# Register loads behind each block's turn, late sums at iterations' ends, rows stored by position, and first splits of layer 1 amid the last gates, in a two-layer routed network on one core

## The chip, the cores and the metric

The kernel runs on one core of a Trainium2 chip. The core has a matmul engine (TensorE, in the profile PE, with PEld for its weight loads), three engines for elementwise work (VectorE = DVE, ScalarE = ACT, GpSimd = POOL), and a queue that only issues transfers (SyncE = SP). ACT and POOL issue transfers too. Each engine executes its instructions in order, and waits for others by semaphores. The metric is the device time of one execution in microseconds, lower is better; the time of the kernel before is the median of 3 runs.

## The reference

The input x has 32 sequences of 128 rows with 512 values; there are two layers, each x + ffn(cond(x)). Cut to what matters:

```python
# layer 0, cond: a mixture of experts with top-2 routing
shared = (silu(x @ sw1.T) * (x @ sw3.T)) @ sw2.T            # hidden width 1024
s      = sigmoid(x @ router_w.T + (t_emb @ router_t_w.T)[seq])
top2   = top_k(s + router_bias, 2)                          # of 8 experts
hidden = (shared + sum(gate_e * gelu(x @ rw1[e].T) @ rw2[e].T)) / 3
# layer 0, ffn: one of 8 experts for each sequence
sel    = argmax(softmax(gelu(hidden[:, -1] @ Wp1 + bp1) @ Wp2 + bp2))
x      = x + hidden + 0.3 * ((gelu(hidden @ W1[sel] + b1[sel]) @ W2[sel] + b2[sel]) @ Wo + bo)
# layer 1, cond: 16 experts by a hash of the token, 256 places each
xk, xr = x + dxprev * maa_k, x + dxprev * maa_r             # dxprev: row before minus row
y      = expert_out[slot];  expert_out = relu(xk_rows @ w_key[e])**2 @ w_value[e]
z      = sigmoid(xr @ w_recept) * y
# layer 1, ffn: a gated recurrence over the 32 sequences (128 rows side by side)
f, i, g = sigmoid(z@wf.T+c@uf.T+bf), sigmoid(z@wi.T+c@ui.T+bi), tanh(z@wc.T+c@uc.T+bc)
c      = f * c + i * g                                       # 32 steps
x      = x + tanh(z @ wo.T + c @ uo.T + bo)
```

## The kernel before

All of it is one program. Matrix products in float32 are made of three matmuls in a reduced format: each operand is split into a high part, a copy on ACT (L64), and a low part, a subtraction on DVE (L65, `split`), and `mm3` (L82) adds high x high, high x low and low x high in PSUM. So every operand passes through ACT and then DVE before PE can use it, and both do this in program order.

The framework schedules the instructions of each engine by priorities and releases; `tc.issue_after(x)` holds an instruction behind instruction x in that schedule, and `behind(pair)` does so for two. `value_load` and `values_load` read a number from SBUF into a register of an engine; it is an instruction on that engine's queue and is shown in no row of busy time. The stages, with the times of the profiled execution:

- 0 to 300 us, shared experts of sequence groups 0 to 3 (8 groups of 4 sequences, 512 columns). `shared` runs 8 chunks of the hidden width for each group: `up` makes two products, `down` adds to 4 accumulators. `mid0` is called after each half of a chunk of group 0 (half steps m = 2n + w) and puts the router's matmuls among them: `cut(m)` says how many of the 32 pieces of x the router has done by then (4 pieces of group 0, 28 that are fetched again by `fetch_r` and split). `seq_bias` computes the routing bias by sequence; its condition `n + w == 1` holds for two half steps, so it runs twice. Then the generators `slots` (places for layer 1's experts) and `choose` (top 2, block tables) advance a step for each chunk from `hook2`. Loads of x and of weights are issued on SP by `fetch`.
- 300 to 548 us, routed experts: 64 full blocks of 128 gathered rows and up to 7 more in conditional pairs (`maybe`, from block 16 on, every sixth block). For block i `r_up` multiplies with a matrix whose column is a register, `first_col(i)`, read by PE from blk_e; `turn_x(i + 1)` transposes the next rows, `r_down(i - 1)` is the second product, `turn_h(i)` the transpose between (L682). The count of used blocks is read by four engines at block 12 (`used`), and each conditional (L702) branches on it. `maybe` reads the columns of its pair in front of the branch.
- 548 to 827 us, shared experts of groups 4 to 7. Beside them `get_o(b)` gathers the two expert rows of sequence b and loads its shared rows (shc) and x, and `combine(b)` adds them up (L793, L794), transposes (L797) and stores the hidden rows. After 24 sequences `policy` picks each one's expert and sorts the sequences by it: seq_i is the sequence at each position, idxw the weight rows.
- 827 to 1431 us, the second product of layer 0 by position. Iteration b runs `up`, `bend` (transpose and gelu) and `down` for two halves of the hidden width, `turn_r`, and for each pair of positions `close` (the product with Wo, new x, and xk). `send_k` and `send_v` transpose and store xk rows and gate rows r = xr @ w_recept to xk_d and v_d, at the row of the sequence, for which SP or ACT reads seq_i into a register (`rows_of`). Weights are gathered on POOL (L906), split on ACT and DVE only where the expert changes (a conditional on a register, L934). The last four sequences are summed in here: `get_o` at b = 3, 6, 9, 12, `combine` at b = 5, 8, 11, 14, both in the middle of the iteration, the second `policy` for positions 24 to 31 at b = 17.
- 1431 to 1809 us, layer 1's experts: 16 experts of 8 weight pieces. `fetch_piece` loads a piece on SP (L1321), `split_piece` splits it, `fetch_rows` gathers an expert's xk rows by slot_t on POOL (L1335), `turn_rows` transposes them (L1348), `use_piece` multiplies; the last piece copies the result on ACT (L1382) and stores it to res_d from ACT's queue (L1384).
- 1809 to 2495 us, the recurrence, 32 steps of about 20.0 us. `get_y(b)` gathers y from res_d on POOL (L1456) and loads r from v_d on SP (L1461); `gate_y` multiplies (L1476) and transposes (L1481). Weights come through `weight` (L1426). After the last step the outputs are finished group by group, without matmuls from 2473.7 us on.

The sequence of each conditional in the routed stage, before:

```python
es = [first_col(i) for i in pairs[n]]
with tc.If(used > pairs[n][0]):
    for i, e in zip(pairs[n], es):
        r_up(i, e)
```

Of the kernel before, what the change touches and what calls it, by code (L numbers as in the profile page):

```python
# [20 lines left out]
P = 128  # L21
# [4 lines left out]
GB = 4  # L26
# [23 lines left out]
def tile_kernel(ctx: ExitStack, tc: tile.TileContext, a: dict, out: bass.AP):  # L50
# [44 lines left out]
    bias_d = dram.tile([E0 * P, 3 * KD], F32, tag="bias", name="bias_d")  # L95
    v_d = dram.tile([N, D], F32, tag="v", name="v_d")
    sh_d = dram.tile([(NG // 2 + 1) * GT, D], F32, tag="sh", name="sh_d")
    o_d = dram.tile([NBLK * P, D], F32, tag="o", name="o_d")
    xk_d = dram.tile([N, D], F32, tag="xk", name="xk_d")
# [31 lines left out]
    seq_i = const.tile([P, NB], I32, name="seq_i")  # L131
    s0_i = const.tile([P, NB], U32, name="s0_i")
# [17 lines left out]
    pad = const.tile([P, 416 // 4], F32, name="pad")  # L150
# [7 lines left out]
    with ExitStack() as sa:  # L158
# [6 lines left out]
        def fetch(src, name):  # L165
            t = raw_p.tile([P, D], F32, tag="raw", name=name)
            nc.sync.dma_start(out=t, in_=src)
            return t

# [35 lines left out]
        def fetch_x(g):  # L205
            if g < NG:
                x_raw[g] = [fetch(a["x"][g][:, k, :], f"xraw_{g}_{k}") for k in range(KD)]
# [68 lines left out]
        with ExitStack() as s0:  # L276
# [32 lines left out]
            fetch_sw(1)  # L309
            ps_acc = s0.enter_context(tc.tile_pool(name="ps_acc0", bufs=4, space=PSUM, **kw))  # L310
# [51 lines left out]
            def seq_bias():  # L362

                ps = ps_r.tile([P, NB, E0], F32, tag="r", name="ps_tb")
                for k in range(KD):
# [7 lines left out]
                    mm(ps, ones, pr, k == 0, k == KD - 1)  # L373
# [4 lines left out]
            def fetch_r(i):  # L378
                g, k = divmod(i, KD)
                if 0 < g < NG:  # L380
                    xrs[i] = fetch(a["x"][g][:, k, :], f"xr_{g}_{k}")
# [165 lines left out]
            def slots():  # L547
# [28 lines left out]
                yield from invert(slot_t, [hi], [lo], NSLOT // P, "st")  # L576
                zero = rtile([P, D], "zero")
# [15 lines left out]
            def cut(m):  # L593
                return min(NR, KD + (NR - KD) * (m - 1) // 15) if m > 0 else 0

            def mid0(n, w):

                if n < KF:
# [3 lines left out]
                    for i in range(cut(m + 1), cut(m + 2)):  # L602
                        fetch_r(i)
                    if n + w == 1:
                        seq_bias()
# [3 lines left out]
            def hook2(g, c):  # L609

                if g == 0:
                    next(steps[0], None)
                    return
                if g == 1 or (g == 2 and c < 5):
# [40 lines left out]
        with s1:  # L655
# [4 lines left out]
            last_up = []  # L660
# [4 lines left out]
            def r_up(i, e=None):  # L665
                if e is None:
                    with tc.issue_after(last_up[0]) if last_up else nullcontext():
                        e = first_col(i)
                x = xb.pop(i)
                pu = ps_u.tile([P, HR], F32, tag="u", name=f"pur_{i}")  # L670
                last_up[:] = [
# [6 lines left out]
            def turn_h(i):  # L678
                u, e = us.pop(i)
                pt = ps_h.tile([P, HR // P, P], F32, tag="t", name=f"pth_{i}")  # L680
                for k in range(HR // P):
                    nc.tensor.transpose(pt[:, k, :], u[:, bass.ts(k, P)], ident)  # L682
# [4 lines left out]
            def r_down(i):  # L687
                h, e = hb.pop(i)
                po = ps_o.tile([P, D], F32, tag="o", name=f"por_{i}")
                mm3(po, lambda q, k: h[:, q, k, :], lambda q, k: r2[:, q, bass.ds(e + k * D, D)], HR // P)  # L690
# [9 lines left out]
            def maybe(n):  # L700
                es = [first_col(i) for i in pairs[n]]
                with tc.If(used > pairs[n][0]):  # L702
                    for i, e in zip(pairs[n], es):
                        r_up(i, e)
# [7 lines left out]
                last_up.clear()  # L712

            for i in range(NFULL + 1):
                if i < NFULL:
# [7 lines left out]
                if i < NFULL:  # L723
                    turn_h(i)
                n, step = divmod(i - FIRST, STEP)
                if i == FIRST - 4:
                    engines = (nc.tensor, nc.scalar, nc.vector, nc.sync)
                    used = nc.values_load(
                        used_i[0:1, 0:1], engines=[x.engine for x in engines], min_val=NFULL, max_val=NBLK
                    )  # L730
# [38 lines left out]
        for kind, i in BIAS.items():  # L769
            nc.sync.dma_start(out=bias_d[:, bass.ts(i, KD)], in_=a[kind][:, KD * D :])  # L770
# [42 lines left out]
        def policy(b0, b1, sm, ps_t, room=None):  # L813
# [69 lines left out]
            nc.vector.tensor_scalar(idxw[:, b0:b1], srow, part_f, None, ALU.add)  # L883
# [900 lines left out]
```

## Time and profile before

| | us |
|---|---|
| median of 3 runs | 2500.74 |
| lowest and highest | 2498.92, 2503.20 |
| profiled execution, own time | 2497.22 |
| its span | 2495.5 |
| PE busy | 2434.5 |
| PEld, DVE, ACT, POOL busy | 2060.7, 1326.8, 1034.5, 412.3 |

The profile comes from one execution; its mean granted TensorE clock is 0.991 of full speed. A row of the waits names an engine, the work that waited and what ended the wait, with total, count and longest in us. A row of the timeline gives start and length of a run of like instructions, and in brackets the idle time in front of it. A row of the windows gives the busy time of each engine in a stretch, and behind it the granted clock.

### The profile page before, as it was taken

To read this page: it belongs to the slowest core of one execution; us is meant where nothing else is said; L and a number is where in the kernel's file an instruction comes from. 1 tells how busy PE (TensorE), PEld (TensorE's weight loads), DVE (VectorE), ACT (ScalarE), POOL (GpSimd) and SP (SyncE) were. 2 spreads that over 40 slices of the span, in tenths; PEclk is the share of its full clock that TensorE was granted. 3 is DMA by queue.
4 is the path that set the end of the run, shared out by engine and by line. 5 is a ranking of instruction groups with operands and counts; after the bars stand their busy time and mean duration, and the time that the engine had idled before them with its cause. 6 is when DMAs were issued, how large, how long until landed. Compare 5 with 4: busy or idle time off the path is not lost.

```text
span 2495.5 us, 36566 instructions
## 1 busy us (share of the span) xinstructions
PE 2434.5 (98%) x12932; PEld 2060.7 (83%) x12932; DVE 1326.8 (53%) x2265; ACT 1034.5 (41%) x1826; POOL 412.3 (17%) x462
## 2 busy tenths in 40 slices
PE   8999999999999899999999999999999999999996
PEld 5788888888888788888888889999978888888885
DVE  7897644456567344454454486766642333333336
ACT  4444533343224454454454376666532222222214
POOL 1000022221233233322222100000010000000003
PEclk9999999999999999999999999999999999999998
DMA  5545544457564333341342487777431111111017
GB/s 181 168 126 169 187 161 161 163 185 238 183 215 165 115 120 127 102 153 57 118 146 94 152 295 232 222 228 234 155 125 39 38 40 42 43 42 38 26 70 280
DMA packets 193402, 351.62 MB, mean 141 GB/s; under 512 B 37504, under 2 KB 72368, under 8 KB 190144
## 3 DMA queue, kind: packets, MB, share of 16 engines
q1 hardware_dynamic: 142080, 246.51, 29.9%
q0 software_dynamic: 36448, 75.95, 10.3%
q10 hardware_dynamic: 14688, 26.75, 3.0%
q8 instruction: 108, 1.77, 0.3%
q14 instruction: 78, 0.64, 0.1%
HBM read 373.94 MB, written 88.65 MB: 185 GB/s over the span
## 4 chain that ended last, share of the span: by engine, by line
PE 49%; DVE 2%; DMA 1%; ACT 0%; issue 0%; POOL 0%; SPq 0%; POOLq 0%; DVEq 0%; ACTq 0%
PE phD L82 7%; PE ps_c L82 7%; PE ps_f L82 7%; PE ps_i L82 7%; PE poD L82 7%; PE poF L82 3%; PE po L82 3%; PE pb L82 2%; PE pv L82 1%; PE ptF L1481 1%; PE ptC L1488 1%; PE ptD L1348 0%; DMA v_d<-r 0%; DMA rawD<-in_w_value_dram 0%; PE ptB L1196 0%
## 5 line engine op out<-in xcount | busy, mean ns | idle before, releaser
L65 DVE TENSOR_TENSOR wD<-rawD,wD 128x1024 fp32r<-128x1024 f32 x128 | 156.4, 1229 | 80.8 <-ACT wD L64 80.7
L82 PE MATMUL p<-xhl,swu 128*128 128x512 f32 x768 | 188.7, 397 | 6.5 <-ACT xhl L64 6.5
L82 PE MATMUL phD<-xe,wD 128*128 128x256 f32 x1536 | 186.9, 282 | 2.0 <-DVE hf L1367 2.0
L82 PEld LDWEIGHTS phD<-xe,wD 128*128 128x128 f32 x1536 | 186.0, 190 | 3.3 <-issue 2.2
L82 PE MATMUL p<-xhl,kept_u 128*128 128x512 f32 x768 | 184.3, 394 | 0.7 <-DVE kept_u L65 0.7
L82 PE MATMUL poD<-wD,hD 128*128 128x512 f32 x768 | 181.3, 392 | 0.0
L82 PEld LDWEIGHTS p<-xhl,swu 128*128 128x128 f32 x768 | 144.6, 190 | 36.9 <-ACT xhl L64 6.5
L82 PEld LDWEIGHTS p<-xhl,kept_u 128*128 128x128 f32 x768 | 141.9, 188 | 30.0 <-DVE kept_u L65 1.1
L82 PEld LDWEIGHTS poD<-wD,hD 128*128 128x128 f32 x768 | 142.0, 188 | 28.4
L64 ACT CAST wD<-rawD 128x1024 fp32r<-128x1024 f32 x128 | 133.2, 1047 | 55.4 <-PE poD L82 50.1
L281 POOL DMA_INDIRECT xg<-in_x_rows_dram,blk_t x71 | 67.6, 952 | 454.9 <-PE ptx L291 246.4
L1456 POOL DMA_INDIRECT y<-res_d,gat_i x32 | 30.8, 962 | 573.6 <-DVE r L1476 492.1
L82 PE MATMUL pur<-r,xb 128*128 x792 | 111.5, 291 | 7.2 <-issue 4.2
L82 PE MATMUL por<-r,hbr 128*128 x396 | 108.0, 407 | 1.2 <-ACT hbr L64 1.2
L82 PEld LDWEIGHTS pur<-r,xb 128*128 128x128 f32 x792 | 99.7, 192 | 9.0 <-issue 6.9
L65 DVE TENSOR_TENSOR xb<-ptx,xb 128x512 fp32r<-128x512 f32 x68 | 47.0, 691 | 106.4 <-ACT xb L64 104.7
L82 PE MATMUL poF<-z,wo_hl 128*128 128x512 f32 x384 | 96.4, 399 | 0.0
L82 PE MATMUL ps_f<-wf_hl,z 128*128 128x512 f32 x384 | 96.2, 399 | 0.0
L82 PE MATMUL ps_c<-wc_hl,z 128*128 128x512 f32 x384 | 94.7, 396 | 0.7 <-ACT z L64 0.7
L82 PE MATMUL pb<-rT,Wo_hl 128*128 128x256 f32 x768 | 94.7, 281 | 0.3 <-DVE rT L65 0.2
L82 PE MATMUL acc<-swd,as 128*128 128x512 f32 x384 | 95.0, 392 | 0.0
L82 PE MATMUL pv<-w_recept_hl,xr 128*128 128x512 f32 x384 | 93.1, 391 | 0.5 <-ACTq L934 0.4
(1017 smaller groups left out, 4955.6 us busy)
## 6 DMA issues: line engine op xcount, KB each, us to landing
rawD<-in_w_key_dram SPq DMA_DIRECT2D x64, 512.0 KB, 4.3
rawD<-in_w_value_dram SPq DMA_DIRECT2D x64, 512.0 KB, 4.4
swr<-in_sw_dram SPq DMA_DIRECT2D x120, 256.0 KB, 3.2
o_d<-obr SPq DMA_DIRECT2D x66, 256.0 KB, 2.4
xraw<-in_x_dram SPq DMA_DIRECT2D x32, 256.0 KB, 4.2
rraw<-in_rw_dram SPq DMA_DIRECT2D x32, 256.0 KB, 3.0
xc<-in_x_dram SPq DMA_DIRECT2D x32, 256.0 KB, 3.5
hid_d<-o ACTq DMA_DIRECT2D x32, 256.0 KB, 2.2
```

The lines of the kernel that those rows point to most:

```text
L64: first = nc.scalar.copy(hi, src).ins
L65: done = nc.vector.tensor_tensor(lo, src, hi.bitcast(F32), ALU.subtract).ins
L82: done = nc.tensor.matmul(ps, lhsT=left(hl, k), rhs=right(hr, k), start=start and k + n == 0, stop=stop and 3 * k + n == last,)
L281: nc.gpsimd.indirect_dma_start(out=xg[i], out_offset=None, in_=a["x_rows"], in_offset=bass.IndirectOffsetOnAxis(ap=blk_t[:, i : i + 1], ax ...
L1456: got = nc.gpsimd.indirect_dma_start(out=y, out_offset=None, in_=res_d, in_offset=bass.IndirectOffsetOnAxis(ap=gat_i[:, b : b + 1], axis=0),)
L1481: nc.tensor.transpose(pt[:, k, :], r[:, bass.ts(k, P)], ident)
L1488: nc.tensor.transpose(pt[:, k, :], c[:, bass.ts(k, P)], ident)
```

## The change

- Start: the three loads to bias_d go from the start of the third stage's code (where the schedule issued the first of them at 3.63 us) to group 1, behind the weight loads there. Pieces 0 and 2 of the first x are loaded from ACT's queue. The router's pieces have buffers of their own and are fetched behind the first loads; `cut` starts two half steps later and ends at the same one (13 instead of 15). `seq_bias` runs once, at the end of group 0, and adds its four products on DVE ahead of a single matmul.
- Routed blocks: `know(i)` reads the column of block i behind block i - 1's transposes (`turn_h`), no longer behind its first product; the loads of `used` stand behind the second product and split of the blocks before 12, and those of a conditional's pair inside the branch, each behind the block before it.
- Late sums: `get_o` is issued behind the hid and weight loads of its iteration, `combine` and `policy` go to the end of the iteration, behind the last split and the last transposes; the second policy comes at b = 15.
- Rows by position: `send_k` and `send_v` store at the position's fixed row, with no register. Layer 1's gather list slot_t is corrected for it: `policy` keeps pos_i and moved = (position - sequence) x 128, and `by_position`, at b = 16 and 17, adds to each entry of slot_t the move of its sequence (slot_b). In the recurrence r is loaded from a row that SP reads from pos_i, one load behind the other.
- Seam to layer 1: the pools for its pieces and rows open before the end of the stage before; 6 pieces are fetched and the first rows gathered there, and five pieces are split on ACT and DVE before the last gate products (two of them ahead of the mix of the last positions). On ACT the casts of wc and wi then come ahead of the last two result copies (L1382) in the instruction order.

```diff
+                    if c == KF - 1:
+                        seq_bias()
...
+                    if k > 0:
+                        nc.vector.tensor_tensor(pr, pr, sum_, ALU.add)
+                    sum_ = pr
+                ps = ps_r.tile([P, NB, E0], F32, tag="r", name="ps_tb")
+                mm(ps, ones, sum_, True, True)
...
-                return min(NR, KD + (NR - KD) * (m - 1) // 15) if m > 0 else 0
+                return min(NR, KD + (NR - KD) * (m - 3) // 13) if m > 2 else 0
...
+            def know(i, *behind):
+                with ExitStack() as order:
+                    for ins in behind:
+                        order.enter_context(tc.issue_after(ins))
+                    cols[i] = first_col(i)
...
-                es = [first_col(i) for i in pairs[n]]
+                last_pe.clear()
                 with tc.If(used > pairs[n][0]):
-                    for i, e in zip(pairs[n], es):
-                        r_up(i, e)
+                    for i in pairs[n]:
+                        know(i, *last_pe)
+                        r_up(i)
...
+                if i + 1 < NFULL:
+                    know(i + 1, *last_pe, *(loads[:1] if i == FIRST - 3 else ()))
...
+        def by_position(pool, i):
+            n = D // NB
+            for s in (bass.ts(i, n),):
...
+                nc.vector.tensor_tensor(
+                    room, slot_b[:, s].unsqueeze(2).to_broadcast([P, n, NB]),
+                    iota_b.unsqueeze(1).to_broadcast([P, n, NB]), ALU.is_equal,
+                )
+                nc.vector.tensor_tensor(room, room, moved.unsqueeze(1).to_broadcast([P, n, NB]), ALU.mult)
...
+                nc.vector.tensor_reduce(by, room, AX.X, ALU.add)
+                nc.vector.tensor_tensor(slot_t[:, s], slot_t[:, s], by, ALU.add)
...
-            return t[bass.ds((seq(p, queue) + where(p)[0] * PARTS[0]) * P, P), :]
+            return t[p * P : (p + 1) * P, :]
...
+                with tc.issue_after(last_hid[0]), tc.issue_after(last_w[0]):
+                    get_o(NB - GB + late, cb, 1)
...
-            if 0 <= late < GB and step == 2:
-                combine(NB - GB + late, ps_t)
-            if late == GB and step == 2:
-                policy(PARTS[0], NB, cb, ps_t)
...
                 bend(b + 1, "b")
+                with behind(last_split), tc.issue_after(last_turn[0]):
+                    if 0 <= late < GB and step == 2:
+                        combine(NB - GB + late, ps_t)
+                    if late == GB and step == 0:
+                        policy(PARTS[0], NB, cb, ps_t)
+                    if late == GB and step > 0:
+                        by_position(cb, step - 1)
...
+        AHEAD, RAW, FIRST = 8, 6, 5
+        fetch_rows(0)
+        for p in range(RAW):
+            fetch_piece(p)
+        fetch_rows(1)
+        for p in range(2):
+            with behind(r_done):
+                split_piece(p)
+            fetch_piece(p + RAW)
+        with tc.issue_after(last_piece[0]):
+            store_x1(NB // PB - 1, 1)
...
+        for p in range(2, FIRST):
+            with behind((r_done[0], xr_done)):
+                split_piece(p)
+            fetch_piece(p + RAW)
...
-            nc.sync.dma_start(out=r, in_=v_d[b * P : (b + 1) * P, :])
+            with tc.issue_after(last_r[0]):
+                at = nc.sync.value_load(pos_i[0:1, b : b + 1], min_val=0, max_val=PARTS[part] - 1)
+            last_r[:] = [nc.sync.dma_start(out=r, in_=v_d[bass.ds((at + part * PARTS[0]) * P, P), :]).ins]
```

## The prediction

> **What bounds the kernel now.** I read the page's busy times first, then TensorE's waits, then the timeline and the windows around each wait.
>
> ```profile
> span 2495.5 us, 36566 instructions
> PE 2434.5 (98%) x12932; PEld 2060.7 (83%) x12932; DVE 1326.8 (53%) x2265; ACT 1034.5 (41%) x1826; POOL 412.3 (17%) x462
> ```
>
> TensorE (PE) is busy for all but 61.0 us. Some 22 us of these are the tail after its last matmul at 2473.7, which the change leaves alone. So a gain can come from three places only: the other 39 us of idle time, matmuls that are no longer issued, and matmuls that ran at half clock. The waits, by what PE waited for (total, times, longest):
>
> ```profile
> PE po L82 <- DVE hb_0a L65: 6.7, 1, 6.7
> PE p L82 <- ACT xhl L64: 6.5, 1, 6.5
> PE pur L82 <- issue: 4.2, 1, 4.2
> PE ptD L1348 <- DMA rowsD<-xk_d,slot_t: 2.4, 2, 1.4
> PE ptF L1481 <- DVE r L1476: 2.3, 1, 2.3
> PE phD L82 <- DVE hf L1367: 2.0, 1, 2.0
> PE pur L82 <- PEq L702: 1.9, 1, 1.9
> PE rt L56 <- DVE rwa L359: 1.8, 1, 1.8
> PE ps_tb L56 <- ACT zt L397: 1.7, 1, 1.7
> PE ps_tb L56 <- DVE tbias L374: 0.8, 1, 0.8
> ```
>
> Each is a single event at a seam between stages; the loops themselves show none. The windows of 2 us (columns: busy PE, PE loads, DVE, ACT, POOL; then granted clock, DMA share, GB/s) show a second cost:
>
> ```profile
> 368.00:370.00 2.00, 0.73 (x3) 0.74 (x4) 0.00 (x0) 0.00 (x0) 0.00 (x0) 0.50 0.00 0
> 370.00:372.00 2.00, 2.00 (x12) 2.00 (x11) 0.00 (x0) 0.00 (x0) 0.00 (x0) 0.50 0.00 0
> 844.00:846.00 2.00, 2.00 (x5) 1.61 (x6) 1.24 (x2) 0.00 (x0) 0.83 (x2) 0.50 0.35 121
> 1822.00:1824.00 2.00, 2.00 (x6) 1.47 (x7) 1.29 (x2) 0.00 (x0) 0.99 (x2) 0.50 0.93 329
> ```
>
> After the long waits the granted clock is 0.50 for some 4 to 6 us of busy matmuls. Half of that is lost: 2.3 us after the wait at 369, 2.05 after 844, 1.7 twice between 1435 and 1452, 2.9 after 1820. The wait of 1.91 at 401 set off none.
>
> The timeline (start, length, engine, line; in brackets idle time and what ended it) names the work:
>
> ```profile
> 28.73 1.97 PE L56 MATMUL ps_tb<-pr,ones 128*128 128x256 f32 x8 [1.66 <-ACT zt L397]
> 369.27 5.13 PE L82 MATMUL pur<-r,xb 128*128 x24 [4.23 <-issue]
> 841.63 0.75 DVE L793 SCALAR_TENSOR_TENSOR o<-o,g,shc 128x512 f32<-128x512 f32 x1 [10.02 <-DMA shc<-sh_d]
> 1419.09 0.59 ACT L1207 COPY r<-pv 128x512 f32<-128x512 f32 x1 [8.68 <-PE pv L82]
> 1810.12 0.59 ACT L1382 COPY ob<-poD 128x512 f32<-128x512 f32 x1 [0.77 <-PE poD L82]
> 1812.50 2.00 ACT L64 CAST wi_hl<-raw_wi 128x1024 fp32r<-128x1024 f32 x2
> 1820.54 0.66 PE L1481 MATMUL ptF<-ident,r 128*128 128x128 f32 x4 [2.30 <-DVE r L1476]
> ```
>
> **The change part by part** (gains positive).
>
> A, start and shared groups 0 to 3. The sequence bias is computed once instead of twice and summed on DVE, so 14 of the 16 ps_tb matmul records go: 14 x 0.246 us (1.97 by 8) = 3.4. The waits 1.66, 0.81 and 1.80 stand in front of the early routers and the bias; the routers start two half steps later, so these go: 4.3. The bias_d loads, 1024 descriptors of 16 bytes each and 6.7 us to land, leave SP's first queue, and two of the four first x loads go to ACT's queue: the first split waits for x at 5.75 us, and the four x issues take 1.84 on SP. So the first matmul at 6.46 can come 0 to 1.5 us earlier; I take 0.8, about two of these issues. Against it: the 28 routers run in 13 half steps instead of 15, and the bias (4 products of 0.42, three sums, a copy, about 3.3 us) moves to where DVE is full, 19.05 of 20 us at 60 to 80. Its idle 0.95 there can't hold 3.3, so PE may wait 0 to 2.4; I take 1.5. A = 3.4 + 4.3 + 0.8 - 1.5 = 7.0 (4 to 9.5).
>
> For the two queues the Trainium skill, "DMA: Bandwidth & Descriptors", section "Issuing engines are not separate DMA queues", speaks against a gain: issuing from several engines saves only the issuing time. By it the 0.8 would be at most the 0.9 of two issues, and nothing if the transfers themselves are the limit.
>
> B, register loads of the routed blocks. Before the first conditional (L702) PE's queue held 8 register loads in a row and PE idled 4.23 us; before the second 4 and it idled 1.91; before the third none and 0.30. So one more load costs 0.58. In the new order each load stands behind its own block's transposes. Before the first conditional two are near, about 0.75 to 0.9; at the others about 0.3. That saves 6.44 - 1.45 = 5.0, and the half clock's 2.3 go with the long gap: 7.3 (4 to 8.2). Loads right in front of a block's first matmul are nothing new: in the instruction order most blocks of before have them there, and the blocks between 320 and 360 show no idle PE.
>
> The rule that bears on the 2.3 is in the Trainium skill, "TensorE: Matmul & The Clock Gate", section "What's actually happening": the clock drops after an idle window of about 3.4 us and rises after an equally long busy one. The rows agree at 369 and 844, but at 1448 a gap of 1.98 was followed by half clock too. By the rule the terms for half clock in E and F would be nought, and the forecast 2 to 3 us less.
>
> C, the seam to the per-sequence stage. DVE stood 10.02 us in front of a late sum (L793) whose shared rows had not landed, and the next split, hb_0a, stood behind it: PE lost 6.66, and 2.05 at half clock. Now these loads are issued behind the hid and weight loads, and the sums stand at the end of later iterations (after bend, behind the last split). What ends last instead is the copy chain of hb_0a, whose hi half was ready at 834.8, before PE asked. Left over: up to 3 us where a sum now meets late rows. C = 8 (5 to 8.7).
>
> D, per-sequence stage. Its small waits (0.60, 0.47, 0.43) lie at the late sums and may go or move. Two slot corrections add about 2.3 us of DVE each (three operations on 128x512 at 0.69 and one small); DVE is half busy there. SP loses 64 register operations; rows are now stored by position at fixed addresses. D = 0.5 (-1 to 1.5).
>
> E, the seam to layer 1's experts. Five pieces of its weights are split on ACT and DVE before the last rows, in ACT's idle 8.68 (5 x 1.05 = 5.25 fit). The last xk stores no longer wait for registers on ACT's queue (3.36 for two issues, second at about 1423.2), so the gathers at 1426.70 start some 2 us earlier. That removes the two ptD waits (1.39, 1.05), the wait for hf (1.98), for which ACT was late after six casts in a row, and both half-clock stretches (3.4): 7.8 at most. The pieces took 3.6 to 8.0 us to land; a cast that waits for one holds back r and rows, so I take off 2.3. E = 5.5 (2 to 7).
>
> F, the seam to the recurrence. The casts of wc and wi now stand in front of the two last ob copies on ACT. raw_wi landed 6.9 us after its issue, at 1810.4 and 1811.5, so the last ob, at 1810.12 before, ends about 1812.7 to 1813.7: the store, the y gather behind it and the wait of 2.30 for r grow by 2 to 3 us, less what PE still has to do. F = -2.0 (-3.5 to 0). The r loads now need a register load of the position on SP in each step; SP is idle for most of the 20.0 us step and r is read some 15 us later: nothing. If that cover failed, it would cost up to 0.58 per step.
>
> Sum: 7.0 + 7.3 + 8.0 + 0.5 + 5.5 - 2.0 = 26.3. The profiled execution took 2497.22 (span 2495.5 and 1.72 outside), so 2470.9; it stands 3.5 us below the median of 2500.74, so the forecast is 2474.4. All worst ends give a gain of 10.5 (2490), all best ends 34.9 (2466).
>
> **Rivals.**
> 1. The seams' waits move instead of going: E's casts wait for pieces, F's ob for raw_wi, C's sums for rows, with their half clocks. For it: all these queues are in order. Against: DVE and ACT have idle time beside each. Only A, B and half of C pay, less F's 3: 7 + 7 + 4 - 3 = 15, so 2486 (2481 to 2491).
> 2. The register loads still bunch and DVE in 60 to 180 us holds back the routing: B pays 2, A 2, C and E half: 11, less F's 3, so 2493 (2491 to 2500). For it: DVE 19.8 of 20 us at 140 to 160. Against: the order puts one load per block.
> 3. Slower: SP's register load before each r load of the 32 steps comes late enough to hold PE. It takes the gain away at 26.3/32 = 0.82 us per step; 1.5 us per step gives 2497.2 - 26.3 + 48 + 3.5 = 2522. Against: r of a step is issued two steps of 20 us ahead (at 1821.23 and 1824.83 for steps 2 and 3).
> 4. The removed waits were cover for work which merely moves, and nothing changes: 2499 to 2503.
>
> **How the numbers follow.** Forecast with its own range 2465 to 2481: 0.62; rival 1: 0.22; rival 2: 0.06 (two thirds faster); rival 3: 0.07; rival 4: 0.03. About 0.2% (5 us) is what a measurement can tell from no change. Faster 0.62 + 0.22 + 0.04 = 0.88; same 0.05; slower 0.07. The range holds the forecast and rival 1: 2464 to 2491.
>
> **What would show it.** A: two ps_tb records, no wait for zt. B: waits for pur under 1 us, clock 1.00 at 370. C: no wait for hb_0a. E: the first gather, at 1426.70 before, at about 1402 (the 22.8 of A to D and its own 2 earlier), no half clock at the first poD. F: a longer wait of ptF for r. Wrong would be: a new row of several us in PE's waits, or a step of the recurrence above 20.1 us.

## The result and the profile after

The changed kernel takes 2484.23 us (median of 6 runs, 2478.15 to 2488.72) beside 2499.83 for the kernel before (6 runs, 2496.14 to 2503.20): a ratio of 0.9937, 95% interval 0.992 to 0.9954. That is 0.6% faster and inside the stated range (2464 to 2491), but the gain is 15.6 us where 26.3 were summed. Its profiled execution took 2483.24 (span 2481.5), 14.0 less than that of before.

From the page of the changed kernel, span and busy time:

```profile
span 2481.5 us, 36586 instructions
PE 2429.9 (98%) x12918; PEld 2057.4 (83%) x12918; DVE 1331.9 (54%) x2283; ACT 1035.4 (42%) x1826; POOL 410.5 (17%) x462
```

TensorE is busy for 4.6 us less and idle for 51.6 instead of 61.0, 9.4 less; the two make the 14.0. Its waits after (total, times, longest):

```profile
PE p L82 <- ACT xhl L64: 6.2, 1, 6.2
PE ptD L1431 <- DMA rowsD<-xk_d,slot_t: 3.3, 2, 2.9
PE pl L56 <- DVE pr L865: 3.2, 2, 1.9
PE pth L835 <- DVE o L832: 2.6, 2, 2.3
PE ptF L1564 <- DVE r L1559: 2.1, 1, 2.1
PE rt L56 <- DVE rwa L369: 1.7, 1, 1.7
PE pt_0a L1151 <- ACT ue_0a L1144: 1.4, 1, 1.4
PE pur L82 <- issue: 1.2, 3, 0.7
```

The waits of 6.7 (hb_0a), 2.0 (hf) and 2.5 (ps_tb) of before are gone, and of those of 4.2 and 1.9 (pur) three short ones are left. Three rows are new or larger: ptD, for rows of layer 1; pl, the policy's small matmul, which before waited for nothing at this place; and pth, the transposes of a late sum. The timeline of TensorE places them (start, length, line, operation; in brackets idle time in front and what ended it):

```profile
757.88 0.59 PE L56 MATMUL pl<-pr,ones 128*128 128x192 f32 x2 [1.87 <-DVE pr L865]
824.73 0.66 PE L1151 MATMUL pt_0a<-ident,ue_0a 128*128 128x128 f32 x4 [1.43 <-ACT ue_0a L1144]
926.62 1.08 PE L835 MATMUL pth<-ident,o 128*128 128x128 f32 x4 [2.29 <-DVE o L832]
1115.31 0.43 PE L56 MATMUL pl<-pr,ones 128*128 128x64 f32 x2 [1.29 <-DVE pr L865]
1422.58 0.63 PE L1431 MATMUL ptD<-ident,rowsD 128*128 128x128 f32 x4 [2.89 <-DMA rowsD<-xk_d,slot_t]
1806.46 0.67 PE L1564 MATMUL ptF<-ident,r 128*128 128x128 f32 x4 [2.07 <-DVE r L1559]
```

The windows of 2 us of the same kernel (columns as before: busy PE, PEld, DVE, ACT, POOL, granted clock, DMA share, GB/s) show half clock in places where before had none, or less:

```profile
104.00:106.00 2.00, 2.00 (x7) 1.52 (x6) 1.90 (x5) 1.27 (x3) 0.00 (x0) 0.50 0.35 36
760.00:762.00 2.00, 2.00 (x6) 1.52 (x6) 0.24 (x1) 0.04 (x1) 0.00 (x0) 0.50 0.00 0
928.00:930.00 2.00, 2.00 (x7) 1.52 (x6) 1.15 (x4) 0.34 (x1) 1.07 (x2) 0.56 0.93 234
```

By stage, the gain over the profile of before is, in us (cut at the starts of matmuls: the first and the last pur, the first product of a routed block; the first pu_0a and the last po from hb_0a, the two products of the first position; the last pb, the product with Wo; the first poD, the second product of layer 1's experts):

| step of the forecast | forecast | changed kernel | other runs with that step's code |
|---|---|---|---|
| A start, groups 0 to 3 | 7.0 (4 to 9.5) | 6.6 | 5.1 to 7.0 |
| B register loads | 7.3 (4 to 8.2) | 4.9 | 0.5 to 3.0 |
| third stage (groups 4 to 7) | none | -3.2 | -3.2 to 0.4 |
| C seam to the per-sequence stage | 8.0 (5 to 8.7) | 7.1 | 6.8 to 7.1 |
| D per-sequence stage | 0.5 (-1 to 1.5) | -4.1 | -2.7 to -6.8 |
| E seam to layer 1's experts | 5.5 (2 to 7) | 3.0 | 1.2 to 3.9 |
| F experts, recurrence | -2.0 (-3.5 to 0) | -0.4 | -2.0 to 0.6 |
| sum | 26.3 | 14.0 | |

The last column matters: the stages of one execution differ by 2 or 3 us from another's with the same code. The profile of before is itself at the low end of its runs (2497.22, where their medians are 2499.83 to 2502.9). So A, C, D and E are known to about 1 or 2 us, and B's size is not known better than "0.5 to 5".

### The profile page after: what moved, and what is told of

Same layout as the page of the kernel before. It is cut to its first block, busy times and chain, and to the rows that moved or that the text cites. A ratio compares the mean times of both kernels' runs of the same rounds, so it can differ in the third digit from the quotient of the medians.

```text
span 2481.5 us, 36586 instructions
## 1 busy us (share of the span) xinstructions
PE 2429.9 (98%) x12918; PEld 2057.4 (83%) x12918; DVE 1331.9 (54%) x2283; ACT 1035.4 (42%) x1826; POOL 410.5 (17%) x462
## 4 chain that ended last, share of the span: by engine, by line
PE 52%; DVE 1%; DMA 1%; ACT 0%; issue 0%; POOL 0%; POOLq 0%; DVEq 0%; ACTq 0%
PE phD L82 7%; PE ps_c L82 7%; PE ps_f L82 7%; PE ps_i L82 7%; PE poD L82 7%; PE poF L82 3%; PE po L82 3%; PE pb L82 2%; PE pv L82 2%; PE ptF L1564 1%; PE ptC L1571 1%; PE ptD L1431 1%; PE ptB L1256 0%; PE pr L1176 0%; DMA rowsD<-xk_d,slot_t 0%
```

## The experiments

Each is the changed kernel with one edit, unless said otherwise, and was timed beside the kernel before on the same chip. Ratios are to that kernel. No run undid the start's edits (but for the queue of the first loads) or the rows by position alone, so what these two bring is read from the profiles only.

**The late sums back in the middle of their iterations** (e1). Their loads stay late.

```diff
+            if 0 <= late < GB and step == 2:
+                combine(NB - GB + late, ps_t)
             if b + 1 < NB:
                 bend(b + 1, "a")
...
-                    if 0 <= late < GB and step == 2:
-                        combine(NB - GB + late, ps_t)
```

> The changed kernel with one part undone: the late sums (combine) stand in the middle of iterations 5, 8, 11 and 14 again; their loads stay late and the second policy stays at the iteration's end. In the changed kernel PE waited 2.29 us for the late sum of sequence 28 in front of its transposes at 926.62, with half clock for some 3.4 us of busy matmuls behind it, and 0.26 at 1039.73; before, the same place cost 0.60 and 0.47 at 928.89 and 930.22. Theory (the sum at the end of the iteration is late for the transposes among the gate products): the wait of 2.29 and its half clock go, 0.5 to 1.1 us of small waits come back, and the per-sequence stage is 3 to 3.5 us shorter than in the changed kernel. Rival (the loads are late, not the sum's place): the wait stays at 2 us or more wherever the sum stands, and the time is the same. The wait for hb_0a (6.66 before) stays away by the theory that the late loads are what keep the scheduler from drawing the sum ahead; it comes back, and with it 8 us, if only the sum's place kept it away.

Measured: 2481.13 us, ratio 0.9914 (0.9895 to 0.9933). The per-sequence stage took 568.2, as before (568.0), against 572.2 in the changed kernel; the seam C stayed at 13.4 us (before 20.4). So the theory held. DVE's order of the changed kernel shows why. The transposes pth stand on TensorE amid the gate products pv, in the middle of the iteration, but DVE's sum now comes behind the split of hb_6b, the last one:

```profile
921.76 1.23 DVE L65 TENSOR_TENSOR xr<-dx,xr 128x1024 fp32r<-128x1024 f32 x1 [0.52 <-ACTq L990]
924.15 0.69 DVE L65 TENSOR_TENSOR hb_6b<-hf_6b,hb_6b 128x512 fp32r<-128x512 f32 x1 [1.17 <-ACTq L990]
924.76 0.75 DVE L831 SCALAR_TENSOR_TENSOR o<-o,g,shc 128x512 f32<-128x512 f32 x1
925.72 0.75 DVE L832 SCALAR_TENSOR_TENSOR o<-o,g,o 128x512 f32<-128x512 f32 x1 [0.21 <-DVEq L990]
```

TensorE had finished the products before pth at 924.33 and stood until 926.62. With the sum in the middle this wait is gone, and two small ones of before are back (timeline of TensorE, e1):

```profile
914.93 0.63 PE L1151 MATMUL pt_6a<-ident,ue_6a 128*128 128x128 f32 x4 [0.53 <-DVE ps L1182]
916.26 0.66 PE L1256 MATMUL ptB<-ident,xk 128*128 128x128 f32 x4 [0.47 <-ACT o L837]
```

So the move to the end of the iteration costs 4.0 us by these two profiles: TensorE's waits in the stage add up to 4.96 us in the changed kernel and 3.11 in e1, and its busy time is 566.90 against 564.82, most of that the half clock behind the 2.29. Where the same wait had no half clock behind it (e5, e6, e10, e11), the stage took 570.7 to 571.0, 2.5 to 2.9 more than in e1.

**The loads of the late sums as early as before**, sums at the ends (e2).

```diff
-                with tc.issue_after(last_hid[0]), tc.issue_after(last_w[0]):
-                    get_o(NB - GB + late, cb, 1)
...
+            if 0 <= late < GB and step == 0:
+                get_o(NB - GB + late, cb, 1)
             if b + 1 < NB:
                 bend(b + 1, "a")
```

> The changed kernel with the late sums' loads issued where they were before, in the middle of iteration 3 and with nothing that holds them back; the sums stay at the iterations' ends. The order on PE, DVE and ACT is that of the changed kernel; on SP and POOL the loads of sequence 28 move ahead of a hid load and two weight gathers. Theory (with the sums at the iteration's end, DVE no longer stands in front of hb_0a, and the place of the loads doesn't matter): no wait for hb_0a, the stretch from the first product of sequence 0 to the end of its second is 13 to 14 us as in the changed kernel (20.4 before), and the time is that of the changed kernel within 0.2%. Rival (the loads themselves are in the way of the weights): the stretch grows by 2 to 6 us by a wait for rawB or hid. It also serves as a second sample of the changed kernel elsewhere: by the theory that the half clock near 104 us, behind 32 small transposes, hangs on where in time these fall, it may be there or not; in the changed kernel and in three of the four runs after it, it was.

Measured: 2484.56 us, ratio 0.9928 (0.9905 to 0.995). Seam C is 13.4 us here too. With e1 this shows that either edit alone takes the 7 us, since either takes the sum out of the seam. Before, it stood at 841.63, in front of the split of hb_0a; in e1, with late loads, it stands well behind the seam even in the middle of its iteration, where DVE still waits for the shared rows but TensorE for nothing (timeline of DVE, e1), and in e2 it stands at 924.74.

```profile
880.52 0.75 DVE L831 SCALAR_TENSOR_TENSOR o<-o,g,shc 128x512 f32<-128x512 f32 x1 [3.19 <-DMA shc<-sh_d]
```

Made together, the second edit brings nothing at the seam, and the later sum costs what e1 measured.

**Register loads alone**: the kernel before with only the new place of the loads (e3).

```diff
-                es = [first_col(i) for i in pairs[n]]
                 with tc.If(used > pairs[n][0]):
-                    for i, e in zip(pairs[n], es):
-                        r_up(i, e)
+                    for i in pairs[n]:
+                        know(i, *last_pe)
+                        r_up(i)
```

> The kernel before with one part of the change alone: the register loads of the routed blocks each behind the block in front, and those of a conditional's pair inside it. The routed stage (first to last product of the blocks) took 239.2 us before, 234.3 in the changed kernel and 236.9, 237.9, 237.1 and 238.7 in the four runs after it. Theory (step B: the bunched loads cost 4.23 and 1.91 us and a half clock of 2.3): waits at the three conditionals of at most 0.8 each, the clock at full speed around them, and the stage 4 to 6 us shorter than the 239.2 if nothing else in it moves. Rival (what is won there is lost again at the loads of x and the splits near block 54, where ACT stands in front of the blocks' copies): waits of 2 to 4 us near 490 us, and a gain of 0.5 to 2.5. By both, the start and the other stages are those of the kernel before, with its wait for hb_0a of 6 to 7 us; 0.1 to 0.25% faster in all.

Measured: 2498.99 us beside 2501.72, ratio 0.9986 (0.9972 to 0.9999): hardly told from no change. The waits at the first two conditionals went as the forecast had them, 4.23 to 0.70 and 1.91 to 0.51, with the half clock behind the first. But the stage gained only 2.6 us, as the rival had it. Most of the rest went to splits that are late elsewhere in it: TensorE's other waits there grew from 2.1 us to 5.4 (timeline of TensorE, e3).

```profile
315.08 0.58 PE L82 MATMUL pur<-r,xb 128*128 x2 [1.14 <-ACT xb L64]
374.78 1.78 PE L82 MATMUL pur<-r,xb 128*128 x12 [0.70 <-issue]
401.96 1.80 PE L82 MATMUL pur<-r,xb 128*128 x12 [0.51 <-ACTq L710]
501.27 2.00 PE L82 MATMUL por<-r,hbr 128*128 x6 [1.42 <-ACT hbr L64]
504.32 0.50 PE L82 MATMUL pur<-r,xb 128*128 x2 [0.83 <-ACT xb L64]
```

**No early splits at the seam to layer 1** (e4): the five `split_piece` calls ahead of the last gate products are gone, and the ordinary ones take their place.

```diff
-        for p in range(2):
-            with behind(r_done):
-                split_piece(p)
-            fetch_piece(p + RAW)
...
-            for p in range(FIRST, AHEAD):
+            for p in range(AHEAD):
```

> The changed kernel without the five early splits of layer 1's pieces: the pieces are still fetched early, all splits come behind the first rows as before. From the last product with Wo to the first poD the changed kernel took 38.9 us (1399.33 to 1438.21), the kernel before 41.9 (1410.62 to 1452.54). Theory (the early splits are what made the seam shorter): the wait for hf (1.98 before) and a second stretch of half clock (1.7) come back, so 3 to 4 us more than the changed kernel, 42 to 43 us for the stretch. Rival (the early splits give nothing, since the first rows end the wait anyway): the stretch stays at 38.5 to 39.5 us, or gets shorter by up to 1.5 since the rows no longer stand behind casts that wait for pieces.

Measured: 2482.73 us, ratio 0.9915 (0.9896 to 0.9935); the seam E is 32.1 us, against 33.5 with the splits and 36.5 before, a little shorter, as the rival had it; four other profiles with the splits and their loads as in the changed kernel have 32.6 to 33.9, and e5 has 35.3. The wait for hf is back, the one for rows nearly gone (timeline of TensorE, e4):

```profile
1426.27 0.63 PE L1423 MATMUL ptD<-ident,rowsD 128*128 128x128 f32 x4 [0.43 <-DMA rowsD<-xk_d,slot_t]
1439.62 0.60 PE L82 MATMUL phD<-xe,wD 128*128 128x256 f32 x3 [1.56 <-DVE hf L1442]
```

The early splits, with the loads that follow them, thus remove 1.6 us of waiting for hf and bring 2.9 of waiting for rows.

**The loads that the early splits set off, later** (e6). Each early split frees a buffer, and SP loads the next piece into it, 512 KB, while the last rows are stored and gathered. Here the splits stay early, and pieces 6 to 10 are loaded behind the last store of gate rows.

```diff
             with behind(r_done):
                 split_piece(p)
-            fetch_piece(p + RAW)
...
+        with tc.issue_after(last_store[0]):
+            for p in range(FIRST):
+                fetch_piece(p + RAW)
```

> The changed kernel with one queue reordered: pieces 6 to 10 of layer 1's weights are issued on SP behind the last gate rows' store instead of between these stores. In the changed kernel the last xk stores were issued by 1409.80 and the first gather only at 1415.23 (5.4 us; 3.2 before the change), landing took 6.7 us (median), and PE waited 2.89 for the rows. Theory (step E: piece 6, 512 KB at 1408.81, and pieces 7 to 9 compete with the last rows' stores and with the gather): the gather starts 1 to 2 us earlier and lands in 4.5 to 5.5, PE's wait falls to 0 to 1 us and the half clock of 1.5 us behind it may go: 2 to 4 us faster. Rival (the gather waits for the gate rows' store, not for bandwidth): the gather starts at the same distance behind the stores, and PE's wait stays at 2 us or more. Pieces 6 and up come later, so a third outcome is a new wait of a phD or poD for its piece, up to 5 us.

Measured: 2480.98 us, ratio 0.9909 (0.989 to 0.9928). Seam E fell to 28.6 us, 4.9 less than in the changed kernel and 3.5 less than in e4, so the early splits pay once their loads wait; the theory held. The profile's DMA issues around the seam (queue, operation, count, KB each, median us to landing), first of before in 1410 to 1440, then of the changed kernel in 1403 to 1428:

```profile
v_d<-r SPq DMA_DIRECT2D x6, 256.0 KB, 2.9
xk_d<-rows ACTq DMA_DIRECT2D x2, 256.0 KB, 2.8
rowsD<-xk_d,slot_t POOLq DMA_INDIRECT x8, 4.9
```

```profile
rawD<-in_w_key_dram SPq DMA_DIRECT2D x4, 512.0 KB, 5.8
v_d<-r SPq DMA_DIRECT2D x5, 256.0 KB, 4.8
xk_d<-rows ACTq DMA_DIRECT2D x2, 256.0 KB, 4.7
rowsD<-xk_d,slot_t POOLq DMA_INDIRECT x6, 6.7
```

Stores and gathers took 1.8 to 1.9 us longer beside the pieces. The first gather itself was no earlier against the last pb products: it started 15.9 us behind the start of their run (1399.33), before 16.1 (1410.62). Timelines of POOL and SP, the changed kernel:

```profile
1415.19 0.37 SPq L1368 DMA_DIRECT2D rawD<-in_w_key_dram  x1
1415.23 1.18 POOL L1383 DMA_INDIRECT rowsD<-xk_d,slot_t  x1 [20.07 <-DMA v_d<-r]
```

In e6 SP issues only stores there, the gather starts 14.3 us behind the start of the pb run (1402.08), as it does in e4, which has neither the splits nor their loads. TensorE's first transposes find the rows without a wait (0.78 us of one follow at 1424.19), and the half clock behind that wait, 3.4 us of it in the changed kernel, is gone:

```profile
1414.87 8.65 SPq L1269 DMA_DIRECT2D v_d<-r  x4
1416.39 1.64 POOL L1383 DMA_INDIRECT rowsD<-xk_d,slot_t  x1 [18.59 <-DMA x_d<-x]
1422.38 1.03 PE L1432 MATMUL ptD<-ident,rowsD 128*128 128x128 f32 x8
```

**The casts of wi behind the last result copy** (e5), which the change had put in front of it on ACT.

```diff
-                        done = split(pair[:, 0, s], pair[:, 1, s], raw)
+                        with tc.issue_after(last_ob[0]) if name == "wi" and h == 1 else nullcontext():
+                            done = split(pair[:, 0, s], pair[:, 1, s], raw)
```

> The changed kernel with one cast moved: the second cast of wi waits on ACT behind the last result copy of layer 1's experts. In the changed kernel that cast (1796.58, after 2.16 us of waiting for its load) stood in front of both copies (1797.53 and 1798.51), while the last products ended at about 1796.0. Theory (step F: this place holds back the store, the gather of y and so r): the copies come 1.0 to 1.6 us earlier, the wait of 2.07 for r falls to 0.5 to 1.1, and if it falls far enough the half clock behind it (some 2.9 us lost) goes too: 1 to 4.5 us faster. Rival (the end of the wait is set by the transfers, or r's activation and table load on ACT): the wait stays within 0.4 of 2.07 and the time is the same.

Measured: 2486.56 us, ratio 0.9936 (0.9916 to 0.9955). The wait for r falls from 2.07 to 0.52 us, with no half clock behind it, and the next product then waits for c instead (timeline of TensorE, e5):

```profile
1806.88 0.66 PE L1566 MATMUL ptF<-ident,r 128*128 128x128 f32 x4 [0.52 <-DVE r L1561]
1825.60 0.66 PE L1573 MATMUL ptC<-ident,c 128*128 128x128 f32 x4 [3.00 <-DVE c L1601]
```

From the last poD to the last ps_c it takes 634.2 us, against 635.4 in the changed kernel, and the time is no better. By these two profiles the matmuls wait at one place or at the other, for r or for c; what sets the end of the first step was not isolated.

**Two of these together, and the second policy moved too** (e7): e1, e6, and the second policy in the middle of iteration 15.

```diff
+            if late == GB and step == 0:
+                policy(PARTS[0], NB, cb, ps_t)
...
-                    if late == GB and step == 0:
-                        policy(PARTS[0], NB, cb, ps_t)
```

> Three edits on the changed kernel: the late sums in the middle of their iterations, pieces 6 to 10 behind the last gate rows' store, and the second policy in the middle of iteration 15 instead of at its end. Theory: the first two add up (per-sequence stage about 568 instead of 572, seam from the last product with Wo to the first poD about 28.6 instead of 33.5), and PE's wait of 1.3 to 2.3 us for the second policy's pr goes, since it stands in front of gate products only at the iteration's end: 8 to 11 us faster than the changed kernel's profile up to the first poD; 2 to 3 us of that can be given back in the recurrence's first steps, where shorter waits for r were followed by waits of 1.25 to 3.12 for the first state's transposes. Rival (policy's chain over ACT is late wherever it stands): the wait for pr stays above 1 us.

Measured: 2485.74 us, ratio 0.9926 (0.9898 to 0.9955), no better than the changed kernel. The seam was 29.3, but the per-sequence stage took 573.1. The wait for the policy's pr stays above 1 us, as the rival had it, and a wait of 2.95 for ACT is new in front of gate products, at the conditional around the weights' splits (L990; timeline of TensorE, e7). It is in e8 too (2.97); elsewhere this conditional holds TensorE up by at most 0.4. Why was not tried.

```profile
1103.54 0.46 PE L56 MATMUL pl<-pr,ones 128*128 128x64 f32 x2 [1.44 <-DVE pr L865]
1118.55 0.73 PE L82 MATMUL pv<-w_recept_hl,xr 128*128 128x512 f32 x2 [2.95 <-ACTq L990]
```

**And a weight of the recurrence loaded by SP early** (e8): e7, e5, and wf from SP's queue in place of POOL's.

```diff
-            wx["f"] = weight("wf", wx_p, zop, 4, pair=wx_hl["f"], queue=nc.gpsimd)
+            wx["f"] = weight("wf", wx_p, zop, 4, pair=wx_hl["f"])
```

> The kernel of the three edits, with two more at the seam to the recurrence: the second cast of wi behind the last result copy, and wf loaded from SP as soon as a buffer is free, no longer from POOL behind the first gather of y (there it was issued at 1804.37 and its cast began at 1810.33). Theory (the wait for the first state's transposes, 1.25 to 3.12 us in the runs where the wait for r was shorter, hangs on wf): that wait and its half clock go, and the stretch from the end of layer 1's experts to the last product of the recurrence, 634 to 637 us in all runs so far, falls to 631 to 633. Rival (the two loads compete with the gather of y, or the casts of wf stand in front of z's on ACT): the wait for r grows by 1 to 3 us and the stretch stays at 635 or more.

Measured: 2485.36 us, ratio 0.992 (0.989 to 0.9949). TensorE's wait for c is gone, as the theory had it, but the rival was right about the rest: the stretch took 638.3 us. The y gather started only at 1806.39, behind a weight's load, and the wait for r grew to 4.57 (timelines of POOL and TensorE, e8):

```profile
1806.39 0.95 POOL L1539 DMA_INDIRECT y<-res_d,gat_i  x1 [82.56 <-DMA raw_wo<-in_wo_dram]
1811.24 1.12 PE L1567 MATMUL ptF<-ident,r 128*128 128x128 f32 x4 [4.57 <-DVE r L1562]
```

**The two losses removed, nothing else** (e9): the edits of e1 and e6 in one kernel, the second policy left at the end of iteration 15. Beside it, on the same chip, **the changed kernel again** (e10).

> The changed kernel with two edits together: the first late sums back in the middle of their iterations, and pieces 6 to 10 of layer 1's weights issued behind the last store of gate rows; the second policy stays at the end of iteration 15. Theory (the two losses are separate: sums at the ends cost 4 us in the per-sequence stage, the early piece loads 5 us in the seam to the experts): the stage from the first sequence's second product to the last gate product is 568.1, the seam to the first poD 28.6, and the time is about 8 us below that of the changed kernel, 0.988 to 0.991 of the kernel before. Rival (the losses are what keeps later waits short, so that they come back elsewhere, as they did where the second policy moved too): both stages are as short as that, but the stages behind them are longer by as much, and the time is that of the changed kernel, 0.993 of the kernel before.

> The changed kernel as it is, beside the one with the two edits, on the same chip. If the two losses are separate, it is slower than that one by 6 to 10 us; if not, the two agree within 3 us.

Measured, 5 runs each: e9 2477.84 us (2475.28 to 2484.30), ratio 0.9907 (0.9886 to 0.9928); e10 2484.65 (2481.61 to 2487.46), ratio 0.9924 (0.9905 to 0.9944). The means differ by 5.9 us; from the spread of the five and five, the 95% interval of that difference is 1.6 to 10.2. The per-sequence stage took 568.9 us and seam E 28.5, beside 570.7 and 33.9 in e10, and no later stage was longer. So this kernel is faster than the one before and, by that interval, than the changed kernel. That the two losses are separate is shown by the stages, 568.9 here beside 568.2 in e1 and 28.5 beside 28.6 in e6. The times don't show it: the 5.9 lies just below the 6 to 10 that were expected, and the ratio of 0.9907 can't be told from those of e1 (0.9914) and e6 (0.9909). Its profile and the waits that are left in it at these places:

```profile
span 2473.6 us, 36579 instructions
PE 2424.5 (98%) x12918; PEld 2051.4 (83%) x12918; DVE 1330.0 (54%) x2283; ACT 1034.5 (42%) x1826; POOL 411.8 (17%) x462
```

```profile
760.43 0.59 PE L56 MATMUL pl<-pr,ones 128*128 128x192 f32 x2 [1.83 <-DVE pr L865]
1113.34 0.43 PE L56 MATMUL pl<-pr,ones 128*128 128x64 f32 x2 [1.35 <-DVE pr L865]
1419.36 0.62 PE L82 MATMUL phD<-xe,wD 128*128 128x256 f32 x3 [0.78 <-ACT xe L64]
```

**The first x loads on one queue** (e11).

```diff
-                    fetch(a["x"][g][:, k, :], f"xraw_{g}_{k}", nc.scalar if g == 0 and k % 2 == 0 else nc.sync)
+                    fetch(a["x"][g][:, k, :], f"xraw_{g}_{k}", nc.sync)
```

> The changed kernel with the four first loads of x all on SP's queue, as in the kernel before. Theory of the forecast (two of four issues on a second queue save up to 0.9 us in front of the first matmul): it starts 0.3 to 0.9 us later than the 6.17 of the changed kernel. Rival (the loads themselves are the limit, as the Trainium skill says of the engines' queues): it starts within 0.3 us of 6.17. No difference of time is looked for.

Measured: 2484.29 us (2 runs), as e10. The first matmul started at 5.62 us, earlier than in any of the ten profiles with two queues (6.04 to 6.78); the two other profiles with one queue had 6.46 and 5.74. So neither expectation held, and the sign was wrong: the second queue does not help at the start, and by these few profiles seems to cost some tenths. The Trainium skill, "DMA: Bandwidth & Descriptors", section "Issuing engines are not separate DMA queues", said that it saves issuing time at most; the measurement is on that page's side against the forecast's 0.8, and goes beyond it. The cause of the later start was not tried.

## Why the forecast was right in sign and too high

The sum landed inside the stated range because that range also held rival 1: 2484.23 lies outside the forecast's own 2465 to 2481 and inside rival 1's 2481 to 2491. Of the signs that the forecast named, those of A, B and C showed. E's first did not, as the first gather came at 1415.23 and not about 1402, nor F's, as ptF waited less and not longer. And its sign of being wrong, a new row of several us in TensorE's waits, came true in part with pl (3.2 in two waits) and pth (2.6 in two).

**A held.** The 14 records of ps_tb and the waits 1.66 and 0.81 are gone, 5.9 us together. The 1.80 for rwa, DVE's preparation of the router's weights, stayed at 1.67: the router's first matmul came only 0.7 later (19.04 for 18.34) and met it all the same. The early start by a second queue was wrong in sign. DVE did not hold TensorE back for the bias, though, where 1.5 was taken off. What the forecast did not have is the half clock at 104 (about 1.7 us), told of below.

**B: the mechanism was right, the sum not.** The waits at the conditionals fell from 6.44 (4.23, 1.91, 0.30) to 1.62 (0.66, 0.51, 0.45), 4.8 against a forecast of 5.0, and the half clock of 2.3 went too. But the stage as a whole gained 4.9 in one execution and 0.5 to 3.0 in the others, and e3 has 0.14% of the time (3.5 us, with an interval from 0.01 to 0.28%) for this part alone. The failed step is the tacit one that no other wait would come in place of these: splits of gathered rows are late by 0.5 to 1.9 us near 300 and near 490, with half clock near 490 in six of the ten other profiles of the changed kernel or an edit of it. Why these differ so from run to run was not settled.

**The third stage was in no term.** The policy of the first 24 sequences now waits (1.87 at 757.88, and half clock at 760): DVE stands for a gather of expert rows in front of the policy's sum.

```profile
756.14 0.75 DVE L831 SCALAR_TENSOR_TENSOR o<-o,g,shc 128x512 f32<-128x512 f32 x1 [2.46 <-DMA o<-o_d,s_i]
```

The wait came again, at 0.9 to 2.0, in every profile with the whole change or an edit of it but one (e2, none), and not in before or e3. e2 differs by the early loads of the late sums, which come in the stage behind it, so one profile does not make them the cause. From the start of that gather to this sum it is 5.7 us in the changed kernel and 3.4 in e2; why the rows land later is open.

**C held**, 7.1 of 8.0, the most stable figure of all. The late wait is now the copy chain of hb_0a, 1.43, as the forecast said. What it did not see is that one of its two edits would have done.

**D failed in sign**: 0.5 forecast, -4.1 measured. The step "its small waits (0.60, 0.47, 0.43) lie at the late sums and may go or move" priced the move of `combine` by the waits that it removes. It did not ask where the transposes pth of the moved sum stand on TensorE. They stay amid the gate products, ahead of which DVE now has the whole of `bend`'s last split. e1 shows it. The lower bound of -1 was the failed number; it had no row behind it. The second policy's wait for pr (1.29 at 1115.31) came on top of that, and is still there in e1. The correction of slot_t by position showed no wait of its own.

**E failed in one step**: "so the gathers at 1426.70 start some 2 us earlier". They do not, 15.9 us against 16.1: by the trace the first now ends its wait with a store of gate rows, not with the release of ACT. And beside the loads that the early splits set off, the stores and gathers took 1.8 to 1.9 us longer each. The forecast had the collision on the wrong side: it charged 2.3 for casts that wait for pieces, not for rows that wait behind pieces. e6 put a number to it: 4.9 us. In e4 and e6, without these loads, the gather does start 1.8 us earlier, at 14.3.

**F was wrong in size.** The last result copy did come late, by the forecast's 2 to 3 us: it starts 2.7 us after the last poD's start, against 0.4 before. But its store landed in 2.0 us (issued at 1799.13) instead of the 4.66 that the chain of before shows (1810.73), and that cancels it: ptF waits 2.07 instead of 2.30. Why the store landed sooner was not tried. The register loads of the recurrence cost nothing, as forecast: from the first ptF to the last ps_c it is 624.8 us, against 624.7 before. Rival 3 (slower by SP's registers) falls with that.

The time is nearer to rival 1 (2486, waits that move) than to the forecast (2474), and its theme was right: the per-sequence stage took back 4.1, the third stage 3.2, and E fell short by 2.5. Its places were wrong in part; C paid nearly in full, and F cost 0.4.

## To carry to other kernels

When a step moves in program order, follow each engine's part of it: a sum that moves to the end on DVE while its transposes stay in the middle on TensorE makes a wait where none was. Work done early also frees its buffers early, and so starts the next loads early: price what those meet. Where two edits remove the same wait, try each alone, since the second can only cost.

## What the runs showed of the hardware that was not expected

**Half clock at the same wait in some executions and not in others.** In front of pth TensorE stood 2.25 to 2.29 us in seven profiles. Behind it the granted clock fell in two, the changed kernel (0.56 to 0.58) and e4 (0.50), and was 1.00 in the other five, e2, e5, e6, e10 and e11. At 757.88 a gap of 1.87 was followed by it in the changed kernel; gaps of 1.83 to 1.94 at the same place in e6, e9 and e10 were not. The Trainium skill, "TensorE: Matmul & The Clock Gate", section "What's actually happening", has the clock drop after an idle window of about 3.4 us, and says that the window runs freely. The second part fits these runs, in which the same gap falls either way; the first does not, as gaps well below 3.4 us brought half clock.

**Half clock without a gap.** Behind 32 transposes of 16 columns, which keep TensorE busy by the profile, the clock fell in the changed kernel (its timeline):

```profile
100.69 2.15 PE L419 MATMUL ps_z<-ident,zt 16*128 16x16 f32 x32
```

The clock was at 0.50 in 104 to 106 (the window shown above). It fell behind them in e1, e3, e4, e6, e8 and e11 too, and not in before, e2, e5, e7, e9 and e10, with the same 32 transposes in each. It costs about 1.7 us, worked out from the granted clock of 0.93, 0.50 and 0.72 in the three windows from 102 to 108. That such small transposes count as idle is a guess; that it depends on the moment fits the runs.

Both make single profiles differ by some us with the same code. A part worth 2 or 3 us, like B in most of these profiles, can't be sized from one profile of each kernel.
